# A fixed tracing order for three engines in the last stage of a two-layer transformer kernel

## Chip, cores and metric

One core of a Trainium2 chip runs the whole program in one launch. The metric is the device time of one execution in microseconds (us). A measurement of this kernel can tell about 0.2% from no change.

## What is computed

The input is x, 2 sequences of 2048 tokens with 256 features, in f32. Two layers follow each other, each of the form x = x + attention(layernorm(x)) + ffn(layernorm(x)).

```
xn = _layernorm(x)
x = x + _L0_attn_ref(xn, ...) + _L0_ffn_ref(xn, ...)     # causal attention; 8 routed experts (top 2) and 2 shared ones
xn = _layernorm(x)
x = x + _L1_attn_ref(xn, Wq, Wk, Wv, Wo) + _L1_ffn_ref(xn, ...)
# _L1_attn_ref: softmax(causal(Q K^T / 16)) V Wo
# _L1_ffn_ref: a router weight per token; the 255 tokens of a sequence with the largest weights go through
#   a 16-head attention block among themselves and a gelu MLP; the other tokens keep x
```

The change touches only the second attention and what is interleaved with it.

## The kernel before

**Stages.** The tokens lie in eight blocks of 512 (`x_blocks`), four for each sequence ("batch 0" and "batch 1"). The program runs layer 0's attention, the routed experts, then the shared experts of layer 0 (beside which layer 1's side work of batch 0 runs), then layer 1's attention. That last stage is the one in question: from 1129.8 us to the end.

**Order of the work.** The instructions are traced in some order, and when the `TileContext` closes, its scheduler lays out each engine's queue. It prefers what was traced earlier, but goes by its own estimate of when an instruction's inputs are there: one whose input it holds to be late is overtaken by others that were traced behind it. Only data dependences and hand-written edges bind it: `order` (L106) means "behind that instruction on the same engine", `wait` (L107) a true wait. On the chip each engine then takes its queue strictly in order.

**Main work: `attention` (L236 to L349).** It goes over 32 tiles of 128 query rows, `in_turn` (L352): (0,0) to (0,15), then (1,15) down to (1,0). A tile (b,i) has i/4+1 (rounded down) chunks of 512 key columns, the last one narrower.
- `scores` (L245): for each chunk two TensorE matmuls (L255) into a bank "sc" or "tr" by turns, two banks of each; VectorE scales the chunk into `row` and takes its maximum (L266). After the last chunk: `nmx` (L272, VectorE), the exponential over the whole row (L274, ScalarE), and `inv` (L276, VectorE), which waits for the exponential.
- `turn` (L298): for each chunk GpSimd parts the 32-bit words into two planes (L305) and a DMA transposes them (L307, SP's queue). The transposed planes are put together by a `join`: one copy on VectorE (L285) and one on ScalarE (L286). Joins are put off: each is due 5 pieces later or more (`LAG`), but `if len(joins) == 4: join(*joins.pop(0)[1:])` (L309) traces the oldest at once when four are open. For every tile of four chunks that is this very tile's first chunk, directly behind its own planes and transposes.
- `average` (L313), about three chunks of work behind: matmuls of the joined chunk with the values (L320), and at the tile's end VectorE adds into x (L330).
- `project_q1` (L1457) makes the queries of a block of 512: eight matmul passes (L1462) and two evacuations, one on VectorE and one on ScalarE. These, and most of the side work, share the two banks "mm".

**Side work.** A chunk's scores or a chunk's average is a piece; after each piece `beside` (L134) adds 1.25 to a credit and traces one step of the side work for each whole unit. A step is what a generator does between two `yield`s. In this stage the side work is: `write_back(0)` (L1363: eight times a load of 256 rows of `gain`, one buffer, and two steps later an add to x on VectorE, L1372), `side1(1)`, `write_back(1)`. `side1(1)` is the feed-forward part of batch 1: `prepare` (L858: `moments`, L205 to L214; `layernorm`, L227, four ScalarE operations for each block; transposes, L233; value products, L876), `route` (L917: five rounds of a threshold search, each a count over 2048 weights on VectorE, L954 and L956, and a tiny matmul, L962; then 0/1 matrices, L1021, and matmuls with them, L1031), and `chosen_block` (L1055: a norm, L1089; position angles, L1130 to L1152; a transposed mask through DRAM, L1162 and L1173; a loop over 16 units, each with scores of two heads on TensorE, L1246, softmax on VectorE and ScalarE, L1251 to L1258, transposes, L1267, evacuated to `wide`, and after every second unit L1281 on VectorE and L1284 on TensorE; then the output product, L1323, and the MLP, L1338 and L1350). `behind` (L116) puts a step's SP instructions behind the main work's last SP instruction, and a GpSimd instruction behind VectorE's last `row`.

**The order of tracing, where it matters below.** Counting credits and `yield`s through the code gives where each step is traced. Engines in brackets; SC is a chunk's scores, AVG a chunk's average, numbered tile.chunk.

```
A  step 25-28: moments of blocks 4..7, one block after each of AVG(0,5).1, SC(0,8).0, SC(0,8).1, SC(0,8).2, then
   rsqrt [VectorE], L227 [ScalarE], L233, L876 [TensorE]; only then AVG(0,6).0
B  SC(0,12).3 | nmx, exp, inv, planes, transposes | join (0,12).0 | AVG(0,11).0..2 with found/digit, L954 of round 2,
   L956 [VectorE] traced between them | SC(0,13).0 | L962 of round 2.    Tile (0,13) with rounds 3, 4: likewise
C  SC(0,14).3 | ... | join (0,14).0 | AVG(0,13).0..3 with slots, L1021 x4 [VectorE] | SC(0,15).0 | L1031
D  SC(0,15).3 | ... | join (0,15).0 | L1462 x8 | AVG(0,14).0..3 with L1048 x16 [VectorE] | SC(1,15).0..2 | L1089.. |
   L1077 | SC(1,15).3 | ... | join (1,15).0 | AVG(0,15).0 | angles [VectorE], Sin [ScalarE] | AVG(0,15).1 | L1162 |
   AVG(0,15).2 | L1162, L1162 | ...
E  unit u of the 16: [L1281 and L1284 of the units before, if u is even] L1267 of u-1, L1246 of u, then one main piece
   (none after 3 of the 16, and a narrow one after 2)
F  join (1,14).0 before unit 0; join (1,13).0 behind unit 8; join (1,12).0 before L1462 and L1323
```

Of the kernel before, what the change touches and what calls it, by code (L numbers as in the profile page):

```python
# [50 lines left out]
def transformer_kernel(ctx: ExitStack, tc: tile.TileContext, a: dict, out: bass.AP):  # L51
    nc = tc.nc
# [53 lines left out]
    order = mybir.DependencyInfo(mybir.DependencyClass.NoSync, mybir.DependencyReason.DATA)  # L106
# [9 lines left out]
    def behind(i):  # L116
        if i.engine == mybir.EngineType.Pool and mybir.EngineType.DVE in main:
            tc.add_manual_dep(i, main[mybir.EngineType.DVE].name, wait, reason="no burst of DMAs")
        elif (i.engine == mybir.EngineType.SP or held[0]) and i.engine in main:
            tc.add_manual_dep(i, main[i.engine].name, order, reason="not ahead of its turn")  # L120

    def step():
        while side:
            traced = nc.cur_bb.bb.instructions
            n = len(traced)
            got = next(side[0], step)
            for i in nc.cur_bb.bb.instructions[n:]:
                behind(i)
            held[0] = got == HOLD
            if got is not step:  # L130
                return
            side.pop(0)
# [617 lines left out]
    with ExitStack() as moe:  # L750
# [54 lines left out]
        for at, t in enumerate(planned):  # L805
            product, activated = run(t)
            if at >= len(planned) // 3:
                for dst, src in (next(coming, (None, None)),):
                    if dst is not None:
                        i = nc.scalar.dma_start(dst, src)  # L810
# [661 lines left out]
    def before_tile1(b, i):  # L1472
        while b not in ready:
            step()
        if (b, i) == in_turn[S // P + 1]:
            finished.add(0)

    attention(att, in_turn, project_q1, values1, before_tile1)
    while side:
        step()  # L1480
    for g in range(NB):
        nc.sync.dma_start(
            out[g * 512 : (g + 1) * 512, :].rearrange("(j p) d -> p j d", p=P), x_blocks[g]
        )
# [61 lines left out]
```

## Time and profile before

| | us |
|---|---|
| median of 3 runs (1513.61 to 1515.64) | 1515.09 |
| profiled execution, its own time | 1515.69 |
| its span (first to last instruction) | 1514.0 |
| last stage: first L1462 to the last L320 | 1129.8 to 1509.2 |

The profile is one execution. Busy times are for each engine; PE is TensorE, DVE VectorE, ACT ScalarE, POOL GpSimd. The views that are used are the page's first lines, the busy time of each engine by stretches of time (with the clock granted to TensorE), and the timelines of TensorE, VectorE and ScalarE, in which a bracket at the end of a line is the idle time before the instruction and what ended it. A timeline counts a matmul of f32 as two passes (x2).

### The profile page before, as it was taken

What the parts mean: (1) busy time and instruction counts of PE and PEld (TensorE: products, weight loads), DVE (VectorE), ACT (ScalarE), POOL (GpSimd) and SP (SyncE); (2) the same over time, 40 slices, a digit from 0 to 9 for tenths busy, and PEclk for the clock granted to TensorE, in tenths of its full rate; (3) what the DMA queues carried; (4) which work ended last, traced back from release to release, by engine and by line L of the source; (5) the groups of instructions that cost most, each with busy time, mean ns of one, the idle gap of its engine ahead of it and who ended that gap; (6) DMA issues with size and microseconds to landing.
All of it is one profiled execution on the core that took longest, in us unless ns stands there. A gap on an engine that the chain in (4) does not pass through costs nothing.

```text
span 1514.0 us, 17838 instructions
## 1 busy us (share of the span) xinstructions
PE 1455.0 (96%) x5796; PEld 1032.3 (68%) x5796; DVE 695.7 (46%) x2068; ACT 440.3 (29%) x831; POOL 407.7 (27%) x597
## 2 busy tenths in 40 slices
PE   6999999998999999999999999999999998999998
PEld 4566666667888888886565656666675765676665
DVE  6347433342222222222433447767556468666344
ACT  2443343332111111111112121125614433344233
POOL 3554776522111111101201222122013123421132
PEclk9999999999999999999999999999999999999999
DMA  4844665575887989873101010220005345621154
GB/s 151 262 113 115 173 147 130 140 154 147 228 224 222 274 237 292 225 218 94 34 18 39 29 56 25 87 71 29 0 21 125 90 87 115 134 51 23 35 118 102
DMA packets 288528, 182.99 MB, mean 121 GB/s; under 512 B 190928, under 2 KB 263376, under 8 KB 288432
## 3 DMA queue, kind: packets, MB, share of 16 engines
q1 hardware_dynamic: 252608, 133.90, 35.8%
q10 hardware_dynamic: 28192, 27.06, 5.8%
q0 software_dynamic: 7632, 20.86, 4.4%
q8 instruction: 48, 0.79, 0.2%
q14 instruction: 48, 0.39, 0.1%
HBM read 93.14 MB, written 45.14 MB: 91 GB/s over the span
## 4 chain that ended last, share of the span: by engine, by line
PE 29%; issue 10%; DVE 7%; POOL 3%; DMA 2%; ACT 2%; POOLq 0%; ACTq 0%; DVEq 0%; SPq 0%
PE ps_tr L1413 6%; PE ps_sc L1413 6%; PE ps_pv L1432 5%; POOL planes L305 3%; DMA across<-planes 2%; PE ps_mm L1284 2%; PE ps_mm L1246 1%; DVE x L1443 1%; PE ps_sc L255 1%; PE ps_mm L876 1%; PE ps_mm L1267 1%; PE ps_pv L320 1%; PE ps_mm L1350 1%; DVE row L266 1%; PE ps_tr L255 1%
## 5 line engine op out<-in xcount | busy, mean ns | idle before, releaser
L305 POOL COPY planes<-row 128x512 uint16<-128x512 uint16 (+3 forms) x320 | 167.1, 569 | 298.9 <-ACT row L274 289.2
L286 ACT COPY pT<-across 128x512 uint16<-128x512 uint16 (+3 forms) x160 | 106.1, 677 | 217.6 <-DMA across<-planes 206.7
L255 PE MATMUL ps_sc<-xnT,qT 128*128 128x512 f32 (+3 forms) x384 | 162.4, 544 | 0.5 <-ACT qT L624 0.5
L781 DVE SCALAR_TENSOR_TENSOR hid<-ps_tr,be,act 128x256 f32<-128x256 f32 (+1 forms) x144 | 61.0, 465 | 186.7 <-PE ps_tr L772 181.7
L1402 POOL DMA_INDIRECT ya<-sorted_y,place x64 | 62.3, 973 | 307.5 <-DVE x L1443 224.3
L780 ACT ACTIVATE act<-ps_sc,be 128x256 f32<-128x256 f32 (+1 forms) x144 | 58.8, 459 | 283.3 <-PE ps_sc L772 283.3
L320 PE MATMUL ps_pv<-v,pT 128*128 128x256 f32 x544 | 128.3, 381 | 6.1 <-ACT pT L286 4.7
L772 PE MATMUL ps_sc<-xT,rw 128*128 128x256 f32 (+1 forms) x576 | 129.5, 368 | 1.6 <-POOL xT L765 1.6
L320 PE MATMUL ps_pv<-vg,pT 128*128 128x256 f32 x544 | 125.1, 381 | 5.4 <-ACT pT L286 5.3
L772 PE MATMUL ps_tr<-xT,rw 128*128 128x256 f32 (+1 forms) x576 | 129.4, 367 | 0.0
L765 POOL COPY xT<-xs 128x512 uint16<-128x512 uint16 (+1 forms) x72 | 49.2, 728 | 293.3 <-DMA xs<-sorted_x 270.7
L788 PE MATMUL ps_pv<-rw,hid 128*128 128x256 f32 x544 | 124.9, 382 | 0.0
L1413 PE MATMUL ps_sc<-xnT,sw 128*128 128x512 f32 x256 | 121.9, 594 | 1.7 <-PEq L816 1.7
L1413 PE MATMUL ps_tr<-xnT,sw 128*128 128x512 f32 x256 | 122.0, 593 | 0.0
L320 PEld LDWEIGHTS ps_pv<-vg,pT 128*128 128x128 f32 x544 | 101.4, 189 | 29.7 <-ACT pT L286 10.3
L320 PEld LDWEIGHTS ps_pv<-v,pT 128*128 128x128 f32 x544 | 101.3, 190 | 28.2 <-ACT pT L286 8.2
L1432 PE MATMUL ps_pv<-sw,hid 128*128 128x256 f32 x512 | 117.5, 380 | 0.0
L772 PEld LDWEIGHTS ps_sc<-xT,rw 128*128 128x128 f32 x576 | 105.3, 190 | 15.4 <-POOL xT L765 2.0
L772 PEld LDWEIGHTS ps_tr<-xT,rw 128*128 128x128 f32 x576 | 105.1, 190 | 13.2
L788 PEld LDWEIGHTS ps_pv<-rw,hid 128*128 128x128 f32 x544 | 99.0, 189 | 19.5 <-DVE hid L781 5.9
L1432 PEld LDWEIGHTS ps_pv<-sw,hid 128*128 128x128 f32 x512 | 96.6, 190 | 18.8 <-issue 6.2
L1420 ACT ACTIVATE act<-ps_sc,sb 128x512 f32<-128x512 f32 x64 | 43.9, 686 | 219.5 <-PE ps_sc L1413 206.4
(332 smaller groups left out, 1964.7 us busy)
## 6 DMA issues: line engine op xcount, KB each, us to landing
rw<-in_rw SPq DMA_DIRECT2D x108, 512.0 KB, 4.5
sorted_x<-zero ACTq DMA_DIRECT2D x13, 768.0 KB, 6.4
sorted_y<-y SPq DMA_DIRECT2D x32, 256.0 KB, 4.1
be<-biases SPq DMA_DIRECT2D x36, 132.0 KB, 4.3
table<-xn SPq DMA_DIRECT2D x8, 514.0 KB, 3.6
x<-in_x SPq DMA_DIRECT2D x8, 512.0 KB, 6.6
gains<-zero ACTq DMA_DIRECT2D x8, 512.0 KB, 3.6
gain<-gains SPq DMA_DIRECT2D x16, 256.0 KB, 2.7
```

The lines of the kernel that those rows point to most:

```text
L255: product = nc.tensor.matmul(ps[:, :w], lhsT=qT[:, dc, (i % 4) * P : (i % 4 + 1) * P], rhs=xnT[g0 + k][:, dc, :w], start=(dc == 0), stop=( ...
L286: nc.scalar.copy(words[:, :, 0], flat[:, w : 2 * w]),
L305: nc.gpsimd.tensor_copy(planes[:, h * w : (h + 1) * w], halves[:, :, 1 - h])
L320: product = nc.tensor.matmul(pv[:, :D], lhsT=turned[k][:, j : j + P], rhs=values[g0 + k][:, j // P, :D], start=(c + j == 0), stop=(c + j = ...
L765: nc.gpsimd.tensor_copy(words[:, :, :, 1 - k], xs[:, 2 * k : 2 * k + 2, :])
L772: nc.tensor.matmul(ps[:, k * n : (k + 1) * n], lhsT=we_in[:, dc, (h + k) * P : (h + k + 1) * P], rhs=xT[:, dc, :], start=(dc == 0), stop=( ...
L780: activated = nc.scalar.activation(act, p1[:, at], AF.Silu, bias=b1[:, hc])
L781: nc.vector.scalar_tensor_tensor(hid[:, h + k, :], p2[:, at], b2[:, hc], act, op0=ALU.add, op1=ALU.mult)
L788: product = nc.tensor.matmul(po[:, r, :], lhsT=hid[:, hc, r * P : (r + 1) * P], rhs=w3[:, hc, :], start=(hc == 0), stop=(hc == 3),)
L1402: nc.gpsimd.indirect_dma_start(out=ya, out_offset=None, in_=sorted_y, in_offset=bass.IndirectOffsetOnAxis(ap=place[rank][:, t : t + 1], ax ...
L1413: product = nc.tensor.matmul(ps, lhsT=ww[:, dc, hc * P : (hc + 1) * P], rhs=xnT[g][:, dc, :], start=(dc == 0), stop=(dc == 1),)
L1432: product = nc.tensor.matmul(po[:, :D], lhsT=hid[:, hc, j * P : (j + 1) * P], rhs=w["sw3", n][:, hc, :], start=(hc == 0), stop=(hc == 3),)
```

## The change

Around the call of `attention` in layer 1 and the loop that finishes the side work, every instruction traced on TensorE, VectorE and ScalarE gets an `order` edge to the one traced before it on the same engine. GpSimd's and SP's queues get none. No instruction is added, removed or altered.

```diff
+    traced = len(nc.cur_bb.bb.instructions)
     attention(att, in_turn, project_q1, values1, before_tile1)
     while side:
         step()
+    before_it = {}
+    for i in nc.cur_bb.bb.instructions[traced:]:
+        if i.engine in (mybir.EngineType.PE, mybir.EngineType.DVE, mybir.EngineType.Activation):
+            if i.engine in before_it:
+                tc.add_manual_dep(i, before_it[i.engine], order, reason="as traced")
+            before_it[i.engine] = i.name
```

## The prediction, made before the changed kernel ran

> **What bounds the kernel now.** I read first the page's lines on busy time, then busy time by stretch for the last stage, then the timelines of TensorE, VectorE and ScalarE there.
>
> ```profile
> PE 1455.0 (96%) x5796; PEld 1032.3 (68%) x5796; DVE 695.7 (46%) x2068; ACT 440.3 (29%) x831; POOL 407.7 (27%) x597
> ...
> core 0: us, PE busy (x) PEld busy (x) DVE busy (x) ACT busy (x) POOL busy (x), PEclk, DMA share, GB/s
> 1236.10:1281.80 45.70, 40.83 (x170) 26.50 (x171) 39.74 (x126) 13.11 (x17) 13.27 (x25) 0.96 0.50 98
> 1129.80:1509.20 379.40, 358.75 (x1415) 244.20 (x1413) 225.78 (x699) 142.20 (x270) 96.00 (x172) 0.99 0.40 87
> ```
>
> TensorE bounds the stage: busy 358.75 of 379.4 us, so 20.6 us idle. VectorE is near full only where the threshold search lies (39.7 of 45.7). The question is what keeps TensorE fed. The timelines tell:
>
> ```profile
> 1128.03 0.43 DVE L205 BATCH_NORM_STATS2 ln_stats<-x 128x6 f32<-128x256 f32 x1
> ...
> 1135.63 0.17 DVE L214 SCALAR_TENSOR_TENSOR ln_shift<-ln_mv,ln_rstd 128x16 f32<-128x16 f32 x1
> ...
> 1239.37 2.35 DVE L954 TENSOR_SCALAR_CACHE_REDUCE junk<-wrow,value 128x2048 bf16<-128x2048 f32 x1
> ...
> 1244.52 0.46 DVE L285 COPY pT<-across 128x512 uint16<-128x512 uint16 x1 [2.06 <-DMA across<-planes]
> ...
> 1290.88 0.46 DVE L285 COPY pT<-across 128x512 uint16<-128x512 uint16 x1 [4.27 <-DMA across<-planes]
> ```
>
> ```profile
> 1173.03 0.33 PE L233 MATMUL ps_mm<-ident,xn 128*128 128x128 f32 x1 [1.31 <-ACT xn L227]
> ...
> 1273.89 0.25 PE L1031 MATMUL ps_mm<-number,wrow 128*128 128x2 bf16 x4 [3.49 <-DVE wrow L1021]
> ...
> 1386.11 2.32 PE L320 MATMUL ps_pv<-v,pT 128*128 128x256 f32 x10
> 1389.05 0.44 PE L1267 MATMUL ps_mm<-ident,pr 128*128 128x128 f32 x2 [0.62 <-ACT pr L1258]
> ```
>
> The queues are not in traced order, and the departures are fillers. The moments of batch 1 run at 1128 to 1136, but are traced about 40 us later (list A). L954 of round 2 runs while the join (0,12).0 is waited for, though traced behind it (B). By 1388 TensorE has done all averages of tile (1,13), which are traced behind the whole 16-unit loop; at 1389 three units are still open. The chain forbids all of this.
>
> **The change, part by part.** No instruction is added, so the cost is the waits that open where a filler is forbidden. I walked the traced order with the durations of this trace: 1.72 us for a 512-wide piece, `row` 0.65 (rows come 0.61 to 0.69 apart), joins 0.38 and 0.72, exponential up to 2.2, first planes 1.1. From `nmx` to the first join of a four-chunk tile 6.4 us (1238.1 to 1244.5) to 7.2 (1283.6 to 1290.9).
>
> *Gain adds and start.* The eight adds of `write_back(0)` stand in VectorE's order ahead of rows and joins. From an add to the next landing: 2.7 us (1146.7 to 1149.4), or 5.7 where the load lies behind a tile's transposes on SP. Behind a waiting add lie the joins of (0,1) and (0,4), for which L320 waits 1.3 and 3.1, and two evacuations, 1.6 and 0.9: 6.9 us, against 1.4 now.
>
> *A.* Behind SC(0,8).0 VectorE must do three blocks of moments (4 x (0.43+0.17) = 2.4 each), three rows, a join and 14 tiny operations of 0.21: 12.4 us; then ScalarE 0.5. TensorE has 2.15 us of work (SC(0,8).1 and .2) and a 0.9 us bank wait: L233 waits 11.8. After each of the four L233 groups the evacuation (0.69 and queueing) is uncovered, 0.85 each. Together 15.2, against 1.5 now.
>
> *B.* VectorE's round behind the join: 0.55 + 0.95 + 2.35 + 0.15 = 4.0. In round 2, `nmx` comes 4.3 us after SC(0,12).3, the join ends at 11.05, L956 at 15.05. TensorE, after waiting 2.4 for round 1's L956, has three averages and SC(0,13).0, to 9.4: L962 waits 5.65, and SC(0,13).1 and all behind it. Tile (0,13) likewise: 1.9 and 6.2; the masks 2.0.
>
> *C.* `nmx` + 6.8 + 0.4, then 3.6 for the slots (17 operations of 0.21) and 4 x 1.15 for L1021: 15.4 us. TensorE has 7.7 from its averages and SC(0,15).0: L1031 waits 8.9. B and C: 27.0, against 4.9 now (3.49, 1.23, 0.19).
>
> *D.* The join (0,15).0 comes at 8.8, L1048 takes 16 x 0.42, then three rows, two joins and the norm (3.7): hn is there at 24.1, TensorE at 15.1, so L1077 waits 9.1. Then `nmx`, join (1,15).0, 19 angle operations (3.8), Sin and the evacuation: the third L1162 needs a free bank "mm" and waits 8.0; L1203 1.4. Together 18.5.
>
> *E and F.* From L1246 to L1267 the chain is 0.69 + 0.61 + 2 x 0.69 and queueing, 2.9 us; one piece covers 1.72, a piece and L1284 together 3.4. Behind L1267 its own L1246 covers nothing of the next unit's chain. Even units, with L1284 and a piece ahead, wait little; odd ones 0.2 to 0.6 where VectorE is prompt, since queries and rows ran ahead. Over the 16 units the waits are 0.2 to 2.3 where a piece is missing or narrow or L1281 stands behind a row: 13.7. The joins (1,14).0, (1,13).0 and (1,12).0 hold up L1246, L1284 and L1323 by 4.6, 7.9 and 3.2; behind the loop L1316 and L1077 wait 1.8 and 2.4. Together 33.6. D to F: 52, against 7.7 now.
>
> *Tail.* `write_back(1)` is bound as `write_back(0)` is, and each `inv` holds VectorE through its exponential (now 1 to 1.6 us a tile). The trace of before shows no such wait of TensorE; its 4.7 us of idle in the tail are late joins. From below nothing, from above a gain loop of 3 to 6 us for each of eight adds, some 15; I take 6, nearest to what the same loop gave at the start. The idle of before stays.
>
> *GpSimd and SP* are not chained. Their instructions of the side work follow VectorE and main SP instructions as before, so they are late where VectorE is late; that is in the waits above.
>
> Sum: 6.9 + 15.2 + 27 + 52 + 10.7 = 112 us idle, against 20.6: +91.
>
> *The clock.* The granted clock halves after some gaps:
>
> ```profile
> 1276.00:1278.00 2.00, 2.00 (x7) 0.78 (x6) 2.00 (x4) 0.00 (x0) 0.00 (x0) 0.50 1.30 184
> ...
> 1390.00:1394.00 4.00, 3.97 (x22) 3.02 (x21) 2.01 (x6) 1.68 (x5) 0.00 (x0) 1.00 0.00 0
> ...
> 1400.00:1402.00 2.00, 2.00 (x6) 1.64 (x5) 0.00 (x0) 0.00 (x0) 0.00 (x0) 0.50 0.00 0
> ```
>
> The first follows the gap of 3.49 (0.84, 0.50 and 0.80 in three rows of 2 us: 1.7 us lost), the second 2.11 and 0.67 us close together (3.4 lost, 1398 to 1406). The Trainium skill ("TensorE: Matmul & The Clock Gate", Part 1) has it that the rate halves after an idle window of about 3.4 us, so that 2.8 us in two parts would be free; here they were not. My gaps are 3.1, 11.8, 5.65, 6.2, 8.9, 9.1, 8.0, 4.6, 7.9 and 3.2. By the rule the eight above 3.4 us cost 8 x 1.7 = 14; by the rows (mean of 1.7 and 3.4) all ten cost 10 x 2.6 = 26. While TensorE is slow the others catch up and the next wait is shorter, so I count half, 7 to 13, less the 5.1 of now: +2 to +8, taken as +6.
>
> Total +97. The profiled execution takes 1515.7 with a span of 1514.0, 0.6 above the median; 1515.1 + 97 = 1612, say 1613.
>
> **Rivals.**
> 1. *Milder waits.* TensorE runs three chunks behind its joins; if a join at the head of VectorE is waited for little more than now (4.27 at most), B, C, F and the third L1162 lose most of their 51 us, and A, D's norm and E stay: about 1560. For it: in the trace VectorE already stands idle for joins, 18.9 us in all, and TensorE runs on. Against: it runs on with what the chain forbids.
> 2. *Faster.* The scheduler places TensorE's side work by estimates that are too short, so TensorE waits at L1031 and L1267 for what it was given too early; in traced order main pieces lie between. If all 20.6 us of idle and 5.1 of slow clock went: 1489. It decides if the new waits stay under 25.7 us; L233 and L1077 alone bring 20.9. Against it too: L1031 stands behind SC(0,15).0 in the trace of before as well, and waits.
> 3. *Nothing happens*, if the queues were in traced order already: 1515. The moments at 1128 exclude it.
> 4. *Worse*: the late VectorE delays gain loads and GpSimd's gathers, which then hold VectorE: 1660 and more.
>
> **Chances.** My forecast 0.70, rival 1 0.17, rival 4 0.08, rivals 2 and 3 together 0.05. The likeliest case spans 1575 to 1650. The range for 8 in 10 takes in the upper part of rival 1: 1550 to 1655. A measurement of this kernel can tell about 0.2% from no change: faster by more 0.03, within 0.02, slower 0.95.
>
> **What would show it.** Right: TensorE's idle in the stage near 110 us; L205 to L214 between the rows of (0,8) and L233 waiting about 12 us; L962, L1031, L1077, the third L1162 and one L1284 waiting 5 to 9 us; VectorE waiting for `across` and `inv` much more than 18.9 and 12.0 us; more stretches at clock 0.5. Wrong: if TensorE's waits stay under 2 us, VectorE behind the joins had slack I did not see; if the loss is in the tail, the gain loop was mis-sized; if rows of VectorE still stand ahead of their turn, the chain doesn't bind.

## The result and the profile after

The changed kernel takes 1636.54 us (median of 4 runs, 1633.58 to 1636.84), the kernel before 1514.35 beside it (4 runs, 1513.04 to 1515.64). The ratio is 1.0807, with a 95% interval of 1.079 to 1.0824: 122 us slower. The prediction was 1613, or +97.

The page of the changed kernel, its span, busy times and TensorE's granted clock in 40 slices:

```profile
span 1633.9 us, 17861 instructions
...
PE 1484.1 (91%) x5796; PEld 1049.9 (64%) x5796; DVE 704.6 (43%) x2068; ACT 440.2 (27%) x831; POOL 408.2 (25%) x597
...
PEclk9999999999999999999999999999989898989999
```

Each engine has as many busy instructions as before; the 23 more in the first line (17838 before) are not counted as busy. The same 5796 matmuls are busy 29 us longer than before (1484.1 against 1455.0), and the clock falls to 0.8 in four slices of the last stage. Nearly all of it lies in that stage. Busy time by stretch there, columns as in the prediction; the first row is the stretch of the threshold search and the 0/1 matrices (before: 45.70 us), the second the tail behind the MLP, the third the whole stage (before: 379.40):

```profile
1264.90:1330.30 65.40, 47.10 (x172) 30.13 (x172) 36.74 (x121) 13.68 (x18) 12.70 (x25) 0.87 0.25 51
...
1529.80:1629.20 99.40, 80.78 (x283) 53.64 (x281) 41.14 (x127) 30.23 (x52) 26.60 (x49) 0.95 0.41 90
1130.30:1629.20 498.90, 387.41 (x1415) 260.34 (x1413) 238.91 (x727) 142.59 (x270) 96.84 (x172) 0.92 0.30 66
```

The stage is 119.5 us longer. TensorE's idle time went from 20.65 to 498.90 - 387.41 = 111.5 us (+91), its busy time from 358.75 to 387.41 (+28.7). VectorE, which was 87% busy in the search, is 56% busy (36.74 of 65.40): it is no fuller, it stands in its own queue. Its timeline shows how:

```profile
1185.51 0.68 DVE L266 TENSOR_SCALAR_CACHE_REDUCE row<-ps_sc 128x512 f32<-128x512 f32 x1
...
1186.12 0.42 DVE L205 BATCH_NORM_STATS2 ln_stats<-x 128x6 f32<-128x256 f32 x1
...
1188.26 0.66 DVE L266 TENSOR_SCALAR_CACHE_REDUCE row<-ps_tr 128x512 f32<-128x512 f32 x1
...
1447.46 0.46 DVE L285 COPY pT<-across 128x512 uint16<-128x512 uint16 x1 [4.41 <-DMA across<-planes]
1447.81 0.25 DVE L1281 COPY apart<-vs 128x32 f32<-128x32 f32 x2
...
1549.24 0.69 DVE L1372 TENSOR_TENSOR x<-gain,x 128x512 f32<-128x512 f32 x1 [0.55 <-DMA gain<-gains]
...
1559.81 0.69 DVE L1372 TENSOR_TENSOR x<-gain,x 128x512 f32<-128x512 f32 x1 [7.96 <-DMA gain<-gains]
```

The moments, which ran at 1128 to 1136 before, now stand between the rows of tile (0,8), each block of them 2.1 us ahead of the next row. The join (1,13).0 is waited for 4.41 us by VectorE itself; the copy L1281 that TensorE wants takes 0.25 us and stands behind it, though its source `vs` was made by 1388. The waits of TensorE in the stage (us in total, times, longest):

```profile
PE ps_pv L320 <- DVE pT L285: 23.3, 11, 6.6
PE ps_mm L1284 <- DVE apart L1281: 15.3, 6, 8.0
PE ps_mm L233 <- ACT xn L227: 12.3, 1, 12.3
PE ps_mm L962 <- DVE count L956: 7.4, 3, 3.2
PE ps_mm L1077 <- issue: 6.4, 1, 6.4
PE ps_mm L1267 <- ACT pr L1258: 6.3, 8, 2.3
PE ps_mm L1031 <- DVE wrow L1021: 6.2, 4, 3.5
PE ps_mm L1246 <- DVE qm L1241: 5.8, 1, 5.8
PE ps_mm L1162 <- ACT part L156: 3.8, 1, 3.8
```

"issue" in the line of L1077 means that the profile shows no releaser; VectorE's L1097, which makes L1077's input, runs from 1353.2 to 1353.9, and L1077 starts at 1353.7. Every line but the first is a place that the prediction named. The first and largest, L320 behind joins, it named only at the start; 16.6 of the 23.3 us lie in the tail. The same from VectorE's side, first after, then before:

```profile
DVE inv L276 <- ACT row L274: 49.2, 32, 3.4
DVE x L1372 <- DMA gain<-gains: 37.1, 11, 8.2
DVE pT L285 <- DMA across<-planes: 36.9, 10, 4.4
```

```profile
DVE pT L285 <- DMA across<-planes: 18.9, 15, 4.3
...
DVE x L1372 <- DMA gain<-gains: 15.8, 15, 2.2
...
DVE inv L276 <- ACT row L274: 12.0, 14, 1.6
```

This view alone would put the exponential first; no experiment bears that out.

### The profile page after: what moved, and what is told of

Read it like the earlier page. It is cut to its first block, busy times and chain, and to the rows that moved or that the text cites. A ratio compares the mean times of both kernels' runs of the same rounds, so it can differ in the third digit from the quotient of the medians.

```text
span 1633.9 us, 17861 instructions
## 1 busy us (share of the span) xinstructions
PE 1484.1 (91%) x5796; PEld 1049.9 (64%) x5796; DVE 704.6 (43%) x2068; ACT 440.2 (27%) x831; POOL 408.2 (25%) x597
## 4 chain that ended last, share of the span: by engine, by line
PE 28%; issue 13%; DVE 8%; POOL 3%; DMA 2%; ACT 1%; POOLq 0%; ACTq 0%; DVEq 0%
PE ps_tr L1413 6%; PE ps_sc L1413 6%; PE ps_pv L1432 5%; POOL planes L305 3%; PE ps_mm L1284 2%; PE ps_mm L1246 2%; DMA across<-planes 2%; PE ps_tr L255 1%; DVE x L1443 1%; PE ps_mm L876 1%; PE ps_mm L1350 1%; PE ps_mm L1338 1%; ACT pr L1258 1%; PE ps_mm L1267 1%; PE ps_sc L255 1%
## 5 line engine op out<-in xcount | busy, mean ns | idle before, releaser
L320 PE MATMUL ps_pv<-v,pT 128*128 128x256 f32 x544 | 141.3, 411 | 28.4 <-DVE pT L285 23.3
L255 PE MATMUL ps_sc<-xnT,qT 128*128 128x512 f32 (+3 forms) x384 | 163.3, 549 | 1.4 <-ACT qT L156 0.7
L286 ACT COPY pT<-across 128x512 uint16<-128x512 uint16 (+3 forms) x160 | 106.0, 676 | 212.9 <-DMA across<-planes 198.7
L320 PEld LDWEIGHTS ps_pv<-v,pT 128*128 128x128 f32 x544 | 110.9, 208 | 55.5 <-issue 28.0
L320 PE MATMUL ps_pv<-vg,pT 128*128 128x256 f32 x544 | 125.1, 381 | 5.5 <-ACT pT L286 5.5
L320 PEld LDWEIGHTS ps_pv<-vg,pT 128*128 128x128 f32 x544 | 101.6, 189 | 29.7 <-ACT pT L286 11.1
L274 ACT ACTIVATE row<-row,nmx 128x128 f32<-128x128 f32 (+15 forms) x64 | 76.8, 1200 | 160.5 <-DVE nmx L272 155.0
L285 DVE COPY pT<-across 128x512 uint16<-128x512 uint16 (+3 forms) x160 | 75.1, 472 | 95.6 <-DMA across<-planes 95.3
L772 PEld LDWEIGHTS ps_sc<-xT,rw 128*128 128x128 f32 x576 | 105.5, 191 | 15.2 <-POOL xT L765 2.0
```

Of the source, the lines that this page charges most:

```text
L255: product = nc.tensor.matmul(ps[:, :w], lhsT=qT[:, dc, (i % 4) * P : (i % 4 + 1) * P], rhs=xnT[g0 + k][:, dc, :w], start=(dc == 0), stop=( ...
L274: lead(nc.scalar.activation(row[:, :n], row[:, :n], AF.Exp, bias=nmx, accum_out=total))
L285: nc.vector.tensor_copy(words[:, :, 1], flat[:, :w]),
L286: nc.scalar.copy(words[:, :, 0], flat[:, w : 2 * w]),
L320: product = nc.tensor.matmul(pv[:, :D], lhsT=turned[k][:, j : j + P], rhs=values[g0 + k][:, j // P, :D], start=(c + j == 0), stop=(c + j = ...
L772: nc.tensor.matmul(ps[:, k * n : (k + 1) * n], lhsT=we_in[:, dc, (h + k) * P : (h + k + 1) * P], rhs=xT[:, dc, :], start=(dc == 0), stop=( ...
```

## The experiments

Each kernel is the changed one with an edit, and each ratio is to the kernel before, run beside it (medians 1513.3 to 1513.9 us). Differences between two experiments carry some 4 us of uncertainty.

**Which engine's order costs it?** The theory was that of the prediction: VectorE's order makes results late, and TensorE, bound as well, can't turn to other work meanwhile; so the two cost jointly, and either alone far less. Rival A: VectorE's order alone costs nearly all of it. Four kernels bind fewer engines; the one-word edit is the tuple of engines:

```diff
-        if i.engine in (mybir.EngineType.PE, mybir.EngineType.DVE, mybir.EngineType.Activation):
+        if i.engine in (mybir.EngineType.PE,):
```

> Only TensorE is chained. Theory 1 (the waits come from VectorE's and ScalarE's queues, held at their heads by DMAs and exponentials, and TensorE's chain only forbids filling them): VectorE may again take the moments and the counts early and the gain adds late, so the waits at L233, L962 and L320 go and only those of the 16-unit loop stay: 1530 to 1560 us. Rival (TensorE's own order does it: its side pieces stand where their inputs are never in time): 1600 us or more.

Measured 1545.31 us, ratio 1.0204 [1.0178, 1.023]: TensorE's order alone costs 31 us, as expected.

```diff
+        if i.engine in (mybir.EngineType.DVE,):
```

> Only VectorE is chained. Theory 1: VectorE is as late as with all three chains, but TensorE may take other pieces in the gaps: 1535 to 1580 us. Rival A (VectorE's order alone costs it all, nothing is left to fill with): 1610 or more. Rival B (TensorE's order alone): under 1525.

Measured 1612.71, ratio 1.0658 [1.0629, 1.0687]: 99 of the 122 us. Rival A holds in the main, and the theory of a joint cost falls. The waits of TensorE in this kernel:

```profile
PE ps_pv L320 <- DVE pT L285: 15.5, 10, 7.4
PE ps_mm L1284 <- DVE apart L1281: 14.9, 4, 9.7
PE ps_mm L1267 <- ACT pr L1258: 13.1, 7, 2.6
...
PE ps_sc L255 <- DVE row L266: 7.3, 4, 2.7
PE ps_tr L255 <- DVE row L266: 6.1, 2, 4.7
```

TensorE may be ordered by the scheduler here, but its queue is still laid out before the run, by estimates that did not foresee these waits: L1284 waits up to 9.7 us, and even scores (L255) wait, 13.4 us in all, for a late `row`. At L233 the wait is much shorter than in the changed kernel (2.3 against 12.3). VectorE's edges enter the scheduler's estimates for the other two engines as well; what that adds to the 99 us is not separated.

```diff
+        if i.engine in (mybir.EngineType.Activation,):
```

> Only ScalarE is chained. Theory 1: ScalarE stands at joins and behind exponentials, but it is busy under a third of the stage: 1515 to 1530 us. If the exponentials and joins on ScalarE were the cause: 1560 or more.

Measured 1534.7, ratio 1.013 [1.0109, 1.0151]: 21 us, somewhat more than expected.

```diff
+        if i.engine in (mybir.EngineType.DVE, mybir.EngineType.Activation):
```

> VectorE and ScalarE are chained, TensorE is free. Theory 1: 1540 to 1590 us, more than VectorE alone, less than all three (1636.5), since TensorE fills part of the gaps. If TensorE's chain adds nothing: within 0.5% of 1636.5. If TensorE's chain is the whole cost: under 1530.

Measured 1614.68, ratio 1.0668 [1.065, 1.0686]. The forecast of 1540 to 1590 missed: a free TensorE fills little of the gaps. ScalarE's order adds nothing to VectorE's (2 us, inside the uncertainty), and TensorE's adds the last 22. The single costs (31, 99, 21) sum to 151 against 122: they share waits.

**Which of VectorE's instructions?** The next four bind all three engines but leave one kind of instruction out of the chains, so that the scheduler places it. That need not be where it stood before, so each run says what this freedom returns, not what the instruction's waits cost. Names are gathered in a set `loose`, and the loop skips them:

```diff
-        if i.engine in (mybir.EngineType.PE, mybir.EngineType.DVE, mybir.EngineType.Activation):
+        if i.name not in loose and i.engine in (mybir.EngineType.PE, mybir.EngineType.DVE, mybir.EngineType.Activation):
```

The joins (L285 and L286):

```diff
+                loose.add(i.ins.name)      # in turn()'s join, for both copies
```

> All three chains, but the joins' two copies stand outside them (with the edges they had before the change). Theory (the heads of VectorE's and ScalarE's queues are held by joins whose transposes are not there): the waits of L962, L1031, L1246, L1284 at 8 us, L1323 and the third L1162 shrink, some 25 to 40 us less: 1597 to 1612 us. Rival (the order of the other work costs it, the joins only happen to stand at the head): within 8 us of 1636.5.

Measured 1610.94, ratio 1.0646 [1.0622, 1.067]: 26 us come back, as expected. The waits of TensorE (lines of this file; L1286 is L1284, L322 is L320, L234 is L233):

```profile
PE ps_pv L322 <- DVE pT L286: 17.3, 3, 6.6
...
PE ps_mm L1286 <- DVE apart L1283: 9.3, 6, 2.1
```

The longest wait for `apart` falls from 8.0 to 2.1 us: the join was what L1281 stood behind. VectorE's wait for `across` falls from 36.9 to 12.2. What stays of L320's waits are three long ones, which have another cause, the next experiment's: in the changed kernel each is for a join that stands behind an add of `gain`.

The 16 adds of `gain`:

```diff
-            nc.vector.tensor_add(xb, gain, xb)
+            loose.add(nc.vector.tensor_add(xb, gain, xb).ins.name)
```

> All three chains, but the sixteen adds of gain stand outside. Theory: VectorE waits 37 us for gain loads, and TensorE's start (11 us idle) and tail (18.6) come from there: 20 to 30 us less, 1606 to 1617 us. Rival (adds outside, the joins take their place at the head): less than 8 us gained.

Measured 1621.29, ratio 1.071 [1.0686, 1.0733]: 15 us, less than the 20 to 30 expected. Busy time by stretch of this kernel, its start and its tail:

```profile
1130.30:1177.70 47.40, 41.92 (x133) 23.67 (x131) 28.60 (x89) 14.92 (x31) 13.10 (x24) 1.00 0.46 106
1527.40:1618.70 91.30, 79.52 (x282) 53.59 (x280) 40.93 (x126) 30.01 (x52) 27.17 (x49) 0.96 0.46 98
```

The changed kernel needs 54.7 and 99.4 us for the two, so they give back 7.3 + 8.1 = 15.4. Between them this execution (1625.1 us, 4 above its median) took 4.9 us longer than the changed kernel's. Of TensorE's idle time in the two, 11.2 + 18.6 = 29.8 in the changed kernel, 5.5 + 11.8 = 17.3 stays; before it was 6.1.

One reason why less came back shows in the trace: the adds still hold VectorE where the scheduler put them. Its waits for their loads in the stage fell from 37.1 us only to 24.2; before they were 15.8.

```profile
DVE x L1373 <- DMA gain<-gains: 24.2, 13, 3.1
```

The longest wait of TensorE that stays in the tail, 5.1 us, is again for a join behind such an add.

Why some turns of the gain loop are so long is seen on SP's queue in the changed kernel (each line the issuing, of three):

```profile
1552.91 4.00 SPq L307 DMA_TRANSPOSE across<-planes  x3
1557.00 7.59 SPq L1368 DMA_DIRECT2D gain<-gains  x3
```

The add at 1549.24 stands ahead of its tile's `nmx`; then come the exponential, the planes on GpSimd, three transposes on SP from 1552.91, and only behind them, at 1557.00, the next load of `gain`, which has landed at 1559.8. This turn from add to add takes 10.6 us, of which VectorE waits 7.96 with the joins behind it; turns without a tile's transposes ahead of the load take 3.4 to 4.2.

The reciprocals `inv`:

```diff
-            nc.vector.reciprocal(inv, total)
+            loose.add(nc.vector.reciprocal(inv, total).ins.name)
```

> All three chains, but the reciprocal of each tile, which waits for the exponential, stands outside. VectorE waits 49 us at it. Theory: behind it stand mostly a join or a gain add, which wait longer anyway: 3 to 10 us less, 1626 to 1634. Rival (the exponential at VectorE's head is the main cost): 1610 or less.

Measured 1636.44, ratio 1.0798 [1.0763, 1.0834]: nothing comes back, within some 5 us, where 3 to 10 were expected. The run does not take the whole wait away: VectorE still waits 33.5 us for exponentials, 21 times. So 16 of its largest wait's 49 us went, and alone they were worth nothing that shows. That what stands behind `inv` waits for the same exponential through the transposes anyway is the likely reason, but not shown.

The moments and their rsqrt:

```diff
+        at = len(nc.cur_bb.bb.instructions)      # in moments(), around L205 to L214
...
+        loose.update(i.name for i in nc.cur_bb.bb.instructions[at:])
```

> All three chains, but the moments of batch 1 and their reciprocal roots stand outside, so that they may run early. Theory: the wait of 12.3 us at L233 goes, and the half clock behind it: 11 to 15 us less, 1621 to 1626. Rival (the wait at L233 only takes up a delay that comes later anyway): less than 5 us.

Measured 1626.68, ratio 1.0744 [1.0715, 1.0773]: 10 us, a little under the 11 to 15 expected. L233's wait fell from 12.3 to 1.2.

**Do these hide one another?** The single returns sum to 25.6 + 15.3 + 0 + 9.9 = 51 of 122 us. Either the rest lies in other instructions, or each of the four covers for the others. One kernel leaves all four kinds out (the four edits together):

```diff
+        if i.name not in loose and ...      # joins, gain adds, inv, moments
```

> All three chains, with joins, gain adds, moments and the reciprocals of the tiles outside at once. Alone they gave 25.6, 15.3, 9.9 and 0 us. If they are separate costs they add up: about 1585 us. If they hide one another (a join takes the place of a gain add at the head, a reciprocal that of a join), together they give more than the sum: 1555 to 1575. If they overlap the other way (one wait counted twice): 1595 or more.

Measured 1569.13, ratio 1.0362 [1.0343, 1.0381]: 67 us come back, 17 more than the sum. They hide one another, as expected, and 55 us lie elsewhere. The largest waits of TensorE in that kernel are at L1267 (9.8 us), L1077 (8.4), L1284 (7.2) and L962 (6.6): the loop, the norms and the search.

**Main work among itself, or against the side work?** Here only the main work's instructions are chained; what a step traces on any of the three engines is left out (in `beside`, where a step's instructions are gone through):

```diff
+                loose.add(i.name)
```

> Only the instructions of the main work are chained on the three engines; those of the side steps are left as they were before. Theory (the cost is that main work must wait behind side work and the other way round): 1513 to 1540 us. Rival (the main work's own order, joins forced at a tile's end and a reciprocal behind each exponential, costs it): 1560 or more.

Measured 1538.16, ratio 1.0166 [1.0143, 1.019]: the main work's own order costs 24 us, so about 98 of the 122 come from binding the side steps too. Whether that is their order among themselves or against the main work, no run here separates.

The 16-unit loop's steps alone left out:

```diff
+            loose.update(i.name for i in nc.cur_bb.bb.instructions[looped:])
```

> All three chains, but the side steps of the 16-unit loop stand outside on all three engines. The stretch of the loop took 104 us with the chains and 76.5 without. Theory (the loop's units wait for their softmax at fixed places, and L1284 behind a join at the head of VectorE): 15 to 27 us less, 1610 to 1622. Rival (the time lost there is lost to the main work's waits): less than 8 us.

Measured 1612.86, ratio 1.0648 [1.0632, 1.0664]: 24 us come back, as expected, so the loop's order is worth about what the joins' is.

**The half clock.** Over rows of 2 us, (1 - granted clock) x busy time sums to 26.9 us in the stage, against 4.9 before. To see whether that costs time, the changed kernel got 35 matmuls of 128x512 whose results are overwritten, just ahead of six long waits: the first block's L233, L1077, L1246, L1284, and the averages of (1,11) and (1,10).

```diff
+    def keep_busy(bank_of, n):
+        for _ in range(n):
+            nc.tensor.matmul(bank_of, lhsT=ident, rhs=xnT[7][:, 0, :], start=True, stop=True)
...
+            if last_stage and g == BPB and not c:
+                keep_busy(ps, 11)
```

> The changed kernel with 35 idle matmuls of 128x512 (some 30 us of TensorE's time, results overwritten) in six of its gaps: before L233 of block 4, L1077, L1246 of unit 0, L1284 behind unit 8, and the averages (1,11) and (1,10), each a little shorter than the gap. The computation is unchanged. If the half clock behind a gap costs what the clock shows there (some 12 us) and half of it is taken up by later waits: 6 to 11 us less, 1626 to 1631. If later waits take up all of it: 1636.5 within 3 us. If the added matmuls delay the pieces: slower.

Measured 1636.71, ratio 1.0802 [1.078, 1.0824] (5 runs): no change. TensorE's timeline at the first place (L199 are the added matmuls, L240 is L233):

```profile
1188.48 9.61 PE L199 MATMUL ps_mm<-xnT,ident 128*128 128x512 f32 x22
1200.98 0.33 PE L240 MATMUL ps_mm<-ident,xn 128*128 128x128 f32 x1 [2.90 <-ACT xn L232]
```

The added 9.61 us fill most of the wait and cost nothing: it was a wait for others. But the slow clock's sum fell only from 26.9 to 22.8 us. The many shorter gaps stayed, and behind four of the six places a rest of the wait, 1.96 to 2.90 us, was enough for the clock to fall to 0.5 all the same. So this run shows that the fill is free and that 4 us of slow clock are worth nothing that can be measured; what the other 23 are worth it leaves open.

No version came out faster than the kernel before.

## Why the prediction was right, and where it was not

**Direction and mechanism: right.** TensorE starves because VectorE reaches small copies late. The timeline of TensorE, place by place:

```profile
1197.46 2.80 PE L233 MATMUL ps_mm<-ident,xn 128*128 128x128 f32 x8 [12.33 <-ACT xn L227]
...
1268.20 0.38 PE L962 MATMUL ps_mm<-count,others 128*128 128x1 f32 x2 [3.21 <-DVE count L956]
1268.44 7.12 PE L320 MATMUL ps_pv<-v,pT 128*128 128x256 f32 x24
...
1280.06 0.38 PE L962 MATMUL ps_mm<-count,others 128*128 128x1 f32 x2 [2.78 <-DVE count L956]
...
1319.22 0.25 PE L1031 MATMUL ps_mm<-number,wrow 128*128 128x2 bf16 x4 [3.52 <-DVE wrow L1021]
...
1448.12 3.75 PE L1284 MATMUL ps_mm<-wide,apart 128*128 128x256 f32 x8 [8.02 <-DVE apart L1281]
...
1562.62 5.13 PE L320 MATMUL ps_pv<-v,pT 128*128 128x256 f32 x16 [6.57 <-DVE pT L285]
```

| place | predicted | measured |
|---|---|---|
| L233 | 11.8 | 12.3 |
| L1246, L1284, L1323 behind joins | 4.6, 7.9, 3.2 | 5.8, 8.0, 3.2 |
| L1077, third L1162 | 9.1, 8.0 | 6.4, 3.8 |
| L962 | up to 6.2 | 2.8 to 3.2 |
| L1031, longest | 8.9 | 3.5 |
| idle in A | 15.2 | 12.4 |
| idle in B and C | 27.0 | 19.7 |
| idle in D to F | 52 | 49.6 |
| idle at start and in the tail | 6.9 + 10.7 | 11.2 + 18.6 |
| idle, sum | 112 | 111.5 |

The idle of before in D to F is 8.1 us by its stretches, not the 7.7 of the working, which changes nothing. L233, L1284 and L1323 were met within about 0.5 us, but of the five waits that were to be 5 to 9 us only L1077 and L1284 were; L962, L1031 and the third L1162 stayed under 4. L233 is partly luck: the terms given for it, 12.4 + 0.5 - 2.15, make 10.75 and not 11.8, and VectorE took 11.3 us from the first row of (0,8) on but reached that row 2.55 us late, behind a gain add, a block of moments and an add into x. The equal sums are partly luck too: 12.5 us too many in A to F stand against 12.2 too few at the start and in the tail.

**Too large: B and C.** VectorE's side of round 2 came true: L956 ended 15.0 us after SC(0,12).3, against 15.05. But the working let TensorE arrive at full speed. The 24 passes of averages that follow L962 took 7.12 us; in the kernel before the same passes took 5.44:

```profile
1236.50 5.44 PE L320 MATMUL ps_pv<-v,pT 128*128 128x256 f32 x24
```

After the gap the clock is low (0.51 from 1270 to 1272). With that and a longer wait in round 1, TensorE was through SC(0,13).0 after 12.3 us, not 9.4, and waited 2.8 us instead of 5.65. In C the working let L1031 wait for all four L1021. The first L1031 needs only the first: it waited 3.5, the other three 0.9 each, 6.2 in all against 8.9. The four waits of 0.85 behind L233 did not come either: a piece stands between L233 and L876, one step off my count.

**Too small: start and tail, 17.6 against 29.8.** The gain loop was mis-sized. The working let a load land at most 5.7 us after the add before it, and took 6 us for the eight adds of the tail. Three waits of L320, each for a join behind a late gain add, sum to 5.5 + 4.3 + 6.6 = 16.4 us, the last two of them in the tail. What it missed is the circle behind the 10.6 us turn: the add stands ahead of `nmx`, and so ahead of the transposes that its next load is behind on SP. "The idle of before stays" failed too: 13.4 us are other waits, against 6.1 before. Joins, `inv` and adds of x in a fixed order may cost there as in B to F, which I counted only for tiles with side work beside them; free_gains, whose adds still hold VectorE, does not separate this, and it stays open.

**Too small: the clock, +6.** TensorE's busy time grew by 28.7, of which the rows' slow clock accounts for 22; the other 7 are longer matmul records that I can't place. Ten gaps were counted, but many shorter ones slow the clock as well: in keep_busy, with six long waits largely filled, 22.8 us of slow clock remain. The halving of the estimate, "while TensorE is slow the others catch up", keep_busy neither confirms nor refutes. In the accounting of the stage it is the term that was off (28.7 against 6, the whole of the missing 23 us); whether removing it would save time stays open.

**Not foreseen: whose order it is.** The prediction walked TensorE's traced order and took fillers to be what the chain forbids. The run with VectorE's chain alone loses 99 us with TensorE free. The late copies cost by themselves; TensorE's own order adds 22.

**The rivals.** Milder waits (1560) rested on joins being waited for little more than 4.27 us at most. That came true, the longest is 4.4, but what it was to bring did not: L1284 still waits 8.0 behind such a join. There are fewer such waits than before (10 against 15), but they last 3.7 us on average instead of 1.3, and freeing the joins returned 26 us. Faster (1489) falls. Of the worse case, the late gain loads did hold VectorE (15.8 to 37.1 us), at a price of 15 us; GpSimd's gathers appear in no long wait of TensorE. That the chain would do nothing was excluded rightly: the moments moved to where they are traced.

## What to carry to other kernels

Binding an engine to the order of tracing turns each of its waits for a DMA into a wait of all that is queued behind; look for the 0.25 us copy that the bottleneck wants, and for what stands ahead of it. The busiest wait of an engine is not its price. Leaving one kind out of the chain took 16 of 49 us of VectorE's waiting for `inv` away and returned nothing that shows; 25 of 37 us for the transposes returned 26, and 13 of 37 for the loads 15. So free one kind of instruction at a time and then all together, since they cover for one another, and look each time how much of the wait really went. When a loop waits for a load, follow the issuing queue too: the load's own 2.8 us were a quarter of the longest turn, 10.6 us, the rest lay ahead of it on SP.

## What the hardware did that was not expected

Two nearly equal gaps had different effects on TensorE's clock. The gap of 2.78 us before L962 at 1280.06 left it at full speed, one of 2.84 us before 1289.42 halved it for 6 us. The changed kernel by rows of 2 us, the clock third from the end of a line:

```profile
1280.00:1282.00 2.00, 1.94 (x6) 1.09 (x7) 1.00 (x4) 0.00 (x0) 0.00 (x0) 1.00 0.32 110
...
1290.00:1292.00 2.00, 2.00 (x6) 1.64 (x6) 0.30 (x2) 1.63 (x3) 0.48 (x1) 0.50 0.00 0
```

The Trainium skill ("TensorE: Matmul & The Clock Gate", Part 1) has the clock halve after an idle window of about 3.4 us that runs freely, not from the kernel's start. A free-running window would make equal gaps fall differently, as seen here. But 2.84 us is shorter than the window, and in keep_busy the clock fell to 0.5 behind two gaps of only 1.96 us (rows 1360 to 1362 and 1452 to 1454), while gaps of 1.48 and 1.74 left it at 1.00. So the length that the page gives is no safe limit for this kernel.
